# Graph attention layer on one core: where the end of a finished tile stands in the second step, and which engine takes three small operations

## The chip, the cores and the metric

The kernel runs on one core of a Trainium2 chip. A core has five engines with a queue of instructions each: TensorE (PE in the profile; its weight loads are PEld), VectorE (DVE), ScalarE (ACT), GpSimd (POOL) and SyncE (SP), which here only issues DMAs. Every queue is worked in order; the engines wait for one another through semaphores. The metric is the device time of one execution in microseconds (us). Times in nanoseconds are marked ns.

## The reference, cut to what matters

`x` is 3327 x 256, `adj` is 3327 x 3327 and sparse (a few entries in a row). The layer normalises `x`, applies relu, and runs two steps of attention and of diffusion:

```python
def _top_p_attention(X, W1, W2, W3):
    logits = (X @ W1.T @ W2.T) @ (X @ W3.T).T
    probs = softmax(logits)
    # keep the largest entries of a row until they hold TOP_P = 0.9 of its mass
    A = probs * mask
    return A / A.sum(-1, keepdims=True)
R = (S + I) / (S + I).sum(-1, keepdims=True)
for n in range(2):
    A = _top_p_attention(Xa, W1, W2, W3)
    Xf = R @ Xf
    Xa = A @ Xa
    Z = Z + Xf @ U1[n].T + Xa @ U2[n].T
h = X + Z
out = x + (h - h.mean) / sqrt(h.var + 1e-5) * ln_g + ln_b
```

What costs the time is the threshold of the mask: for every row the value above which 90% of the softmax's mass lies, found without sorting.

## The kernel before, in words

The 3327 rows are 26 tiles of 128 (`NT = 26`). Two passes of one loop (`step` 0 and 1) treat every tile; this document calls them the first and the second step. For each tile `t`:

- `weights` (L582 to L610): queries times keys on PE into PSUM, and four `Exp` on ACT (L604, L608, L610) into `e`, 128 x 3328 f32.
- `measured_twice` (L669 to L717, second step): a guess of the threshold, mended twice. Each look at the tile is one pass of ACT over `e` (L633, "ja" in the profile; Relu once and Sign twice, so three passes a tile). Between the passes stand chains of operations on single columns `col(k)` of a small tile `g`: on DVE L685 and L686 after the second pass, L699 and L700 after the third, L716 and L717 at the end; on ACT L687 to L689, L702 to L705, L714; on POOL L690 to L692 and, after the third pass, L697, L698 and L707 to L712. The last six form a ratio of two differences, clamp it and multiply the exponent `col(11)` by it; L714 on ACT uses that.
- `settle` (L725 to L769), DVE: L731 zeroes everything above the guess (a pass over `e` and `e`, with two inputs in SBUF), L736 takes the eight largest of each of 20 segments, L743 and L745 sort out the 40 or 48 largest of these, L750 to L755 find the exact threshold, L765 (L762 in the first and last tile) applies it to `e` and sums; L766 inverts the sum. Then a product of two rows of 40 or 48 elements (L767: on DVE in the first step, on POOL in the second) and its maximum (L769, DVE) go into a record that is only read by a proof at the end.
- `Sums` (L797 to L834): PE transposes `e` in seven parts of four 128 x 128 blocks (L810), ACT copies each part out of PSUM (L812, "eT"), PE multiplies it with the values (L824, "pa").
- `spread` (L1073 to L1090): the sparse diffusion, six matmuls on gathered rows (L911, "pr"; gathers are indirect DMAs issued by POOL, L903) and a closing DVE operation L1086. Its row tile `s1` (four buffers; loaded from memory by L1078) is the tile's result `y` from then on, until it is stored.
- `finish` (L934 to L955, second step): L935 on DVE adds the attention's sum to `y`; L458 and L459 take mean and variance; POOL forms the inverse deviation (L465, L466) and minus mean times it (L943); then POOL adds `bet` to the input's rows `xr` (L945), ACT normalises `y` (L950), POOL multiplies with `gam` (L951) and adds `xr` (L952); SP stores `y` (L955). `xr` has one buffer, which L940 loads.

All these are generators that yield between their pieces. The order of the work is written by hand: `PLAN[1]` (L1104) holds for the second step seven strings, one for each part `k` of a tile's iteration `i`, and each letter advances one generator by one piece: `d` is `settle(i)`, `c` the rest of `settle(i - 1)`, `m` `measured(i + 1)`, `n` the rest of `measured(i)`, `w` `weights(i + 2)`, `q` its start for `i + 3`, `s` `spread(i)`, `g` the gathers for `i + 2`, `f` `finish(i - 2)`, in parts 0 to 3 still `finish(i - 3)`. For the last iterations `LAST` (L1106) replaces the strings. Before the letters of each part the transposes of a part of the sums are put in, after them its matmuls. At the end (L1183) the instructions of PE, ACT, DVE and POOL (POOL from the second step on) are chained in the order of this text, so the plan is the order of execution on each of these engines. SP's queue is not chained: a scheduler orders the DMA issues, and each waits for its own semaphores.

Of the kernel before, what the change touches and what calls it, by code (L numbers as in the profile page):

```python
# [14 lines left out]
ALU = mybir.AluOpType  # L15
# [329 lines left out]
def guess_graph_layer(ctx, tc, x, adj, w1t, w2t, w3t, u1t, u2t, ln_g, ln_b, out, flag):  # L345
# [15 lines left out]
    V, G, S, PE = nc.vector, nc.gpsimd, nc.scalar, nc.tensor  # L361
# [39 lines left out]
    bet = const.tile([P, D], F32, tag="bet", name="bet")  # L401
# [4 lines left out]
    half = const.tile([P, 4], F32, tag="half", name="half")  # L406
# [209 lines left out]
    def guessed(r, g):  # L616

        r["col"] = col = lambda k: g[:, k : k + 1]
        ms = r["ms"]
        S.activation(r["za"], r["za"], AF.Copy, accum_out=r["Z"])  # L620
        S.activation(col(0), r["Z"], AF.Ln)
        S.activation(col(2), col(0), AF.Relu, scale=-0.25, bias=ms(7))
        S.activation(col(2), col(2), AF.Exp, scale=-1.0, bias=con(6))
        S.activation(col(3), col(2), AF.Square, bias=con(3))
        S.activation(col(9), col(3), AF.Exp, scale=ms(3), bias=ms(8))
        return col

    def con(k):
        return one[:, k : k + 1]

    def through(e, f, guess, sign, total):
        ja = scan.tile([P, NP], U8, tag="ja", name="ja")
        S.activation(ja, e, f, bias=guess, scale=sign, accum_out=total)  # L633
# [35 lines left out]
    def measured_twice(r):  # L669
        e, ms = r["e"], r["ms"]  # L670

        col = guessed(r, small.tile([P, 18], F32, tag="g", name="g"))
        S.activation(col(1), col(0), AF.Exp, scale=-1.0, bias=con(5))
        S.activation(col(11), col(2), AF.Square, bias=con(4))
        G.tensor_scalar(col(11), col(11), ms(5), ms(6), ALU.mult, ALU.add)
        G.tensor_scalar(col(5), col(1), OFFSET[1], None, ALU.mult)
        yield
        oa = small.tile([P, 3], F32, tag="oa", name="oa")  # L680
        through(e, AF.Relu, col(9), -1.0, oa[:, 0:1])
        yield
        through(e, AF.Sign, col(9), -1.0, oa[:, 1:2])
        yield
        V.tensor_scalar(col(3), oa[:, 1:2], float(NP), col(9), ALU.add, ALU.mult)  # L685
        V.tensor_scalar(col(4), col(3), 0.5, oa[:, 0:1], ALU.mult, ALU.subtract)  # L686
        S.activation(col(6), col(4), AF.Ln, scale=col(1), bias=con(2))  # L687
        S.activation(col(6), col(6), AF.Exp, scale=col(11))
        S.activation(col(13), col(6), AF.Copy, scale=col(9))  # L689
        G.tensor_scalar(col(14), col(13), col(9), 0.25, ALU.add, ALU.mult)  # L690
        G.tensor_scalar(col(10), col(13), col(5), 1.0, ALU.mult, ALU.add)
        G.tensor_scalar(col(8), col(4), col(1), -1.0, ALU.mult, ALU.add)  # L692
        yield
        through(e, AF.Sign, col(13), -1.0, oa[:, 2:3])
        yield
        d1 = col(17)
        G.tensor_scalar(col(0), oa[:, 2:3], NP - 61.0, BIG, ALU.is_gt, ALU.mult)  # L697
        G.tensor_scalar(col(0), r["Z"], 0.035, col(0), ALU.mult, ALU.add)  # L698
        V.tensor_scalar(col(15), oa[:, 2:3], oa[:, 1:2], col(14), ALU.subtract, ALU.mult)  # L699
        V.tensor_scalar(d1, col(15), col(4), 0.0, ALU.add, ALU.max)  # L700

        S.activation(col(2), d1, AF.Abs, scale=col(1), bias=con(1))  # L702
        S.activation(col(2), col(2), AF.Ln, scale=0.2, bias=col(10))
        S.activation(col(3), d1, AF.Ln, scale=col(1), bias=con(2))
        S.activation(col(2), col(2), AF.Identity, scale=-1.0, bias=col(3))  # L705

        G.tensor_scalar(col(12), col(4), d1, col(1), ALU.subtract, ALU.mult)  # L707
        G.tensor_scalar(col(8), col(8), col(12), None, ALU.mult)
        G.tensor_scalar(col(12), col(12), col(12), 1.0e-12, ALU.mult, ALU.add)
        G.tensor_tensor(col(12), col(12), half[:, 2:3], ALU.pow)  # L710
        G.tensor_scalar(col(12), col(12), col(8), 0.7, ALU.mult, ALU.max)
        G.tensor_scalar(col(11), col(12), 1.5, col(11), ALU.min, ALU.mult)  # L712
        yield
        S.activation(col(3), col(2), AF.Exp, scale=col(11))  # L714
        yield
        V.tensor_scalar(col(6), d1, col(0), BIG, ALU.is_lt, ALU.mult)  # L716
        V.tensor_scalar(col(16), col(3), col(13), col(6), ALU.mult, ALU.add)  # L717
# [7 lines left out]
    def settle(step, t, r):  # L725
        e, col, Z = r["e"], r["col"], r["Z"]
        n = 8 * ROUNDS[step]
        d2 = small.tile([P, 1], F32, tag="d2", name="d2")
        need = small.tile([P, 1], F32, tag="need", name="need")
        w = scan.tile([P, NP], F32, tag="w", name="w")  # L730
        V.scalar_tensor_tensor(w, e, col(16), e, ALU.is_lt, ALU.mult, accum_out=d2)  # L731
        V.tensor_scalar(need, Z, -0.1, d2, ALU.mult, ALU.add)
        yield
        cand = small.tile([P, NSEG * 8], F32, tag="cand", name="cand", bufs=1)
        for s in range(NSEG):
            V.max(cand[:, 8 * s : 8 * s + 8], w[:, s * SEG : min(NP, (s + 1) * SEG)])  # L736
            if s in (NSEG // 2 - 1, NSEG - 1):
                yield
        at = lambda k: rec[:, step, k, t : t + 1]
        V.tensor_reduce(at(0), cand.rearrange("p (s k) -> p s k", k=8)[:, :, 7], AX.X, ALU.max)  # L740
        for k in range(ROUNDS[step]):
            b8 = bb[:, 1 + 8 * k : 9 + 8 * k]
            V.max(b8, cand)  # L743
            if k < ROUNDS[step] - 1:
                V.match_replace(cand, b8, cand, 0.0)  # L745
            if k == 2:
                yield
        b = bb[:, 1 : n + 1]
        cum = small.tile([P, TOPK], F32, tag="cum", name="cum", bufs=1)
        V.tensor_tensor_scan(cum[:, :n], bb[:, :n], bb[:, :n], 0.0, ALU.add, ALU.max)  # L750

        dr = small.tile([P, TOPK], F32, tag="dr", name="dr", bufs=1)
        V.tensor_scalar(dr[:, :n], cum[:, :n], need, None, ALU.is_ge)
        V.scalar_tensor_tensor(cum[:, :n], dr[:, :n], BIG, b, ALU.mult, ALU.add)
        V.tensor_reduce(at(1), cum[:, :n], AX.X, ALU.min)  # L755
        yield
        r["ra"] = ra = small.tile([P, 1], F32, tag="ra", name="ra")
        if t in (0, NT - 1):

            rb = small.tile([P, 1], F32, tag="rb", name="rb", bufs=1)  # L760
            for a, b_, r_ in ((0, FIRST, ra), (FIRST, NP, rb)):
                V.scalar_tensor_tensor(e[:, a:b_], e[:, a:b_], at(1), e[:, a:b_], ALU.is_ge, ALU.mult, accum_out=r_)  # L762
            V.tensor_tensor(ra, ra, rb, ALU.add)
        else:
            V.scalar_tensor_tensor(e, e, at(1), e, ALU.is_ge, ALU.mult, accum_out=ra)  # L765
        V.reciprocal(ra, ra)  # L766
        (G if step else V).tensor_tensor(cum[:, :n], dr[:, :n], b, ALU.mult)  # L767
        yield
        V.tensor_reduce(at(2), cum[:, :n], AX.X, ALU.max)  # L769


# [162 lines left out]
    def finish(t, y, pa, ra):  # L934
        V.scalar_tensor_tensor(y, pa, ra, y, ALU.mult, ALU.add)  # L935
        yield
        mv = spread_of(y)
        yield
        xr = row.tile([P, D], F32, tag="xr", name="xr", bufs=1)
        nc.sync.dma_start(xr, x[t * P : (t + 1) * P])  # L940
        rstd = inverse(mv)
        nm = small.tile([P, 1], F32, tag="nm", name="nm")
        G.tensor_scalar(nm, mv[:, 0:1], rstd, -1.0, ALU.mult, ALU.mult)  # L943
        yield
        G.tensor_tensor(xr, xr, bet, ALU.add)  # L945
        if t == NT - 1:
            V.scalar_tensor_tensor(y, y, mv[:, 0:1], gam, ALU.subtract, ALU.mult)
            V.scalar_tensor_tensor(y, y, rstd, xr, ALU.mult, ALU.add)
        else:
            S.activation(y, y, AF.Identity, bias=nm, scale=rstd)  # L950
            G.tensor_tensor(y, y, gam, ALU.mult)  # L951
            G.tensor_tensor(y, y, xr, ALU.add)  # L952
        yield
        h = min(P, N - t * P)
        nc.sync.dma_start(out[t * P : t * P + h], y[:h])  # L955

# [135 lines left out]
    def refetch(t):  # L1092
# [8 lines left out]


    PLAN = (("mdsssa", "mdsssa", "edawwp", "msda", "mpdea", "gdawwq", "emdgq"),
            ("llcmss", "lnms", "lwwnfd", "lcmdsssg", "fmswqdf", "llmdf", "lmwfd"))  # L1104

    LAST = {NT - 1: ("cfss", "cn", "ndd", "sss", "fddddsf", "f", "f"), NT: ("cf", "", "", "", "ff", "fv", "f"),  # L1106
            NT + 1: ("fv", "f", "", "", "f", "f", "f")}
# [5 lines left out]
    for step in range(2):  # L1113
        sums = Sums(step, live, xw if step else x0, AHEAD[step])

        for i in range(-1, NT + 2):
# [4 lines left out]
            if step == 1 and i == -1:  # L1121
# [5 lines left out]
                n=work["m"],  # L1127
# [9 lines left out]
                b=none, q=none, v=proof() if step and i == NT else work.get("v", none),  # L1137
# [93 lines left out]
```

## Time and profile before

| | us |
|---|---|
| runs: median of three (lowest, highest) | 1406.87 (1405.7, 1407.31) |
| the profiled execution's own time | 1408.79 |
| its span, first to last instruction | 1407.1 |
| DVE busy in the span | 1220.4 (87%) |
| PE busy | 1278.7 (91%) |
| ACT busy | 1105.6 (79%) |
| POOL busy | 989.7 (70%) |
| from 200 to 600, first step, of each 100 us: DVE / PE / ACT / POOL | 96 / 96 / 80 / 70 to 77 |
| from 900 to 1300, second step, of each 100 us: DVE / PE / ACT / POOL | 92 to 94 / 94 to 95 / 94 to 95 / 84 to 87 |
| mean of the granted TensorE clock | 0.974 of full speed |

The profile is that of one execution; 1.7 us of its time lie outside the span. "Busy" is the time in which an engine had an instruction in it, also one that stood still within it. In the listings by time a row gives start, duration, engine, line, operation, tiles (buffer numbers left out) and, where the engine was idle before it, for how long and whose end it then followed. The second step reaches its steady rhythm near 856 us, and keeps it until 1324 us; one tile follows another every 22.2 us.

### The profile page before, as it was taken

The page shows a single profiled execution, that of the slowest core. Times are in us where ns is not written, and L with a number is a line of the kernel's source. Part 1 is how long each engine was busy: PE and PEld are TensorE (multiplying, and loading weights), DVE is VectorE, ACT ScalarE, POOL GpSimd, SP SyncE. Part 2 cuts the span into 40 slices and gives each one's busy share as a digit, 9 for nine tenths or more (in the row PEclk, how much of TensorE's full clock was granted, in tenths as well). Part 3 has the DMA queues.
Part 4 walks back from the last instruction along what each step waited for, and adds up shares of the span by engine and source line. Part 5 has one row for each costly group of instructions (what it writes and reads, how often), then busy time and mean ns, then how long its engine had stood idle before and what let it go on. Part 6 is the DMA issues. An engine that isn't in the chain of part 4 may idle for free.

```text
span 1407.1 us, 22248 instructions
## 1 busy us (share of the span) xinstructions
PE 1278.7 (91%) x6495; PEld 980.9 (70%) x6495; DVE 1220.4 (87%) x3727; ACT 1105.6 (79%) x2423; POOL 989.7 (70%) x1348
## 2 busy tenths in 40 slices
PE   6898999999999999999999479999999999999885
PEld 5545777777777777778786257777777777777664
DVE  6868999999999999998863589999999999999981
ACT  5467887788778788787944689999999999999921
POOL 6214777667667677768862668888888888888832
PEclk9999999999999999999999579999999999999998
DMA  8874454544545445432331202213121221312100
GB/s 284 263 247 126 134 151 133 138 137 135 146 124 148 133 137 152 129 96 73 101 85 57 78 23 79 79 57 90 55 82 58 79 82 54 90 57 79 57 8 22
DMA packets 91203, 149.78 MB, mean 106 GB/s; under 512 B 15265, under 2 KB 58656, under 8 KB 91072
## 3 DMA queue, kind: packets, MB, share of 16 engines
q1 hardware_dynamic: 73616, 105.37, 24.0%
q0 software_dynamic: 16640, 42.69, 12.1%
q8 instruction: 54, 0.88, 0.3%
q14 instruction: 77, 0.63, 0.1%
q10 hardware_dynamic: 816, 0.20, 0.1%
HBM read 120.93 MB, written 27.28 MB: 105 GB/s over the span
## 4 chain that ended last, share of the span: by engine, by line
DVE 51%; PE 24%; ACT 17%; POOL 3%; issue 3%; DMA 1%; DVEq 0%; SPq 0%; POOLq 0%; ACTq 0%
ACT ja L633 11%; DVE e L765 10%; PE pa L824 9%; DVE cand L736 7%; DVE w L731 6%; DVE fm L846 5%; PE pl L600 4%; DVE bb L743 4%; DVE cand L745 4%; PE pt L810 3%; PE pz L988 2%; DVE x L765 2%; ACT eT L812 2%; PE pr L911 1%; ACT e L604 1%
## 5 line engine op out<-in xcount | busy, mean ns | idle before, releaser
L824 PE MATMUL pa<-xw,eT 128*128 128x256 f32 x1352 | 331.9, 387 | 6.6 <-DVE s L935 6.5
L633 ACT ACTIVATE ja<-e,g 128x3328 uint8<-128x3328 f32 x106 | 325.8, 3074 | 0.1
L824 PE MATMUL pa<-x,eT 128*128 128x256 f32 x1352 | 325.2, 382 | 0.0
L824 PEld LDWEIGHTS pa<-xw,eT 128*128 128x128 f32 x1352 | 250.2, 191 | 68.1 <-issue 27.1
L824 PEld LDWEIGHTS pa<-x,eT 128*128 128x128 f32 x1352 | 245.0, 192 | 26.3
L812 ACT COPY eT<-pt 128x512 f32<-128x512 f32 (+1 forms) x364 | 202.1, 556 | 76.6 <-PE pt L810 76.5
L736 DVE MAX8 cand<-w 128x8 f32<-128x168 f32 (+1 forms) x1040 | 251.3, 318 | 0.0
L810 PE MATMUL pt<-ident,e 128*128 128x128 f32 x1144 | 180.7, 278 | 60.6 <-DVE e L765 36.6
L894 POOL DMA_INDIRECT ac<-in_adj,index x130 | 130.7, 1005 | 128.2 <-DVE ms L538 91.2
L810 PEld LDWEIGHTS pt<-ident,e 128*128 128x128 f32 x1144 | 140.7, 144 | 107.3 <-issue 48.1
L903 POOL DMA_INDIRECT xg<-bx,index x130 | 184.8, 1421 | 41.0 <-issue 30.0
L731 DVE SCALAR_TENSOR_TENSOR w<-e,g 128x3328 f32<-128x3328 f32 x44 | 169.1, 3842 | 0.7
L903 POOL DMA_INDIRECT xg<-vx,index x130 | 131.1, 1009 | 45.6 <-issue 33.0
L765 DVE SCALAR_TENSOR_TENSOR e<-e,rec 128x3328 f32<-128x3328 f32 x40 | 156.6, 3915 | 0.7
L911 PE MATMUL pr<-xg,ac 128*128 128x257 f32 (+1 forms) x520 | 139.1, 391 | 11.5 <-DVE s L1086 11.3
L604 ACT ACTIVATE e<-pl 128x832 f32<-128x832 f32 x132 | 113.0, 859 | 36.4 <-PE pl L600 36.3
L911 PEld LDWEIGHTS pr<-xg,ac 128*128 128x128 f32 x520 | 93.9, 195 | 25.1 <-DVE s L1086 11.4
L743 DVE MAX8 bb<-cand 128x8 f32<-128x160 f32 x286 | 92.8, 325 | 6.4
L600 PE MATMUL pl<-after,qT 64*128 64x416 f32 x416 | 96.7, 559 | 0.5 <-ACT qT L528 0.5
L767 POOL TENSOR_TENSOR cum<-dr,bb 128x48 f32<-128x48 f32 x26 | 84.9, 3264 | 15.5 <-DVE rec L755 15.3
L951 POOL TENSOR_TENSOR s<-s,gam 128x256 f32<-128x256 f32 x25 | 92.5, 3701 | 3.2 <-ACT s L950 3.2
L600 PE MATMUL pl<-both,qT 64*128 64x416 f32 x416 | 90.8, 540 | 0.9 <-DVE both L1006 0.9
(259 smaller groups left out, 2210.7 us busy)
## 6 DMA issues: line engine op xcount, KB each, us to landing
at<-in_adj SPq DMA_DIRECT2D x102, 256.0 KB
cx<-ac SPq DMA_DIRECT2D x26, 384.0 KB
ac<-cx SPq DMA_DIRECT2D x26, 384.0 KB
wide<-in_adj SPq DMA_DIRECT2D x10, 832.0 KB
e<-in_adj SPq DMA_DIRECT2D x8, 832.0 KB
bx<-e SPq DMA_DIRECT2D x26, 128.5 KB
own<-bx SPq DMA_DIRECT2D x26, 128.5 KB
x<-in_x SPq DMA_DIRECT2D x13, 256.0 KB
```

The source lines that it names most:

```text
L600: PE.matmul(pl[:, a, :wd], qT[p, :], keys_of(step, a).rearrange("p a b -> p (a b)")[:, c : c + wd], start=True, stop=True)
L633: S.activation(ja, e, f, bias=guess, scale=sign, accum_out=total)
L731: V.scalar_tensor_tensor(w, e, col(16), e, ALU.is_lt, ALU.mult, accum_out=d2)
L736: V.max(cand[:, 8 * s : 8 * s + 8], w[:, s * SEG : min(NP, (s + 1) * SEG)])
L743: V.max(b8, cand)
L765: V.scalar_tensor_tensor(e, e, at(1), e, ALU.is_ge, ALU.mult, accum_out=ra)
L810: PE.transpose(pt[:, j, :], e[:, (j0 + j) * P : (j0 + j + 1) * P], ident)
L812: S.copy(eT[:, :w, :], pt[:, :w, :])
L824: PE.matmul(self.pa, eT[:, c - 4 * k, :], self.xa[:, j, :], start=c == 0, stop=c == NT - 1)
L894: G.indirect_dma_start(out=ac[:, k, :], out_offset=None, in_=rows, in_offset=bass.IndirectOffsetOnAxis(ap=index[:, t, k : k + 1], axis=0), ...
L903: G.indirect_dma_start(out=xg[:, k, :w], out_offset=None, in_=rows, in_offset=bass.IndirectOffsetOnAxis(ap=index[:, t, k : k + 1], axis=0))
L911: PE.matmul(pr[:, :w], ac[:, k, :], own if k == KT - 1 else xg[:, k, :w], start=k == 0, stop=k == KT - 1)
```

## The change

Four edits, all but one in the second step alone:

1. `finish`: the addition of `bet` to `xr` moves from before ACT's normalisation to between the two POOL operations on `y`, and the piece that held the store is joined to the one that normalises.
2. `PLAN[1]`: the last `f` of part 6 goes, so that the next `f`, in part 2 of the next iteration, normalises: ACT's L950 then stands behind the two `w` of that part, and the three POOL operations and the store follow. In part 4 `s` moves ahead of `m`: DVE's L1086 stands before L685 instead of after L686.
3. `measured_twice`: the ratio is formed otherwise. POOL's `col(8)` is now a difference (same count of operations, L692), and the four POOL operations L707 to L710 give way to two on DVE, a difference and a reciprocal, right behind L700. POOL keeps the two clamps.
4. `settle`: the product L767 moves behind the yield, directly ahead of its maximum L769, and is on DVE in both steps. In the first step it was on DVE already; it only moves.

```diff
@@ measured_twice
-        G.tensor_scalar(col(8), col(4), col(1), -1.0, ALU.mult, ALU.add)
+        G.tensor_scalar(col(8), r["Z"], -0.1, col(4), ALU.mult, ALU.add)
         yield
         through(e, AF.Sign, col(13), -1.0, oa[:, 2:3])
         yield
@@
-        G.tensor_scalar(col(12), col(4), d1, col(1), ALU.subtract, ALU.mult)
-        G.tensor_scalar(col(8), col(8), col(12), None, ALU.mult)
-        G.tensor_scalar(col(12), col(12), col(12), 1.0e-12, ALU.mult, ALU.add)
-        G.tensor_tensor(col(12), col(12), half[:, 2:3], ALU.pow)
+        V.tensor_scalar(col(12), col(4), d1, 1.0e-30, ALU.subtract, ALU.add)
+        V.reciprocal(col(12), col(12))
         G.tensor_scalar(col(12), col(12), col(8), 0.7, ALU.mult, ALU.max)
         G.tensor_scalar(col(11), col(12), 1.5, col(11), ALU.min, ALU.mult)
         yield
@@ settle
         V.reciprocal(ra, ra)
-        (G if step else V).tensor_tensor(cum[:, :n], dr[:, :n], b, ALU.mult)
-        yield
+        yield
+        V.tensor_tensor(cum[:, :n], dr[:, :n], b, ALU.mult)
         V.tensor_reduce(at(2), cum[:, :n], AX.X, ALU.max)
@@ finish
-        G.tensor_tensor(xr, xr, bet, ALU.add)
         if t == NT - 1:
+            G.tensor_tensor(xr, xr, bet, ALU.add)
             V.scalar_tensor_tensor(y, y, mv[:, 0:1], gam, ALU.subtract, ALU.mult)
             V.scalar_tensor_tensor(y, y, rstd, xr, ALU.mult, ALU.add)
         else:
             S.activation(y, y, AF.Identity, bias=nm, scale=rstd)
             G.tensor_tensor(y, y, gam, ALU.mult)
+            G.tensor_tensor(xr, xr, bet, ALU.add)
             G.tensor_tensor(y, y, xr, ALU.add)
-        yield
         h = min(P, N - t * P)
         nc.sync.dma_start(out[t * P : t * P + h], y[:h])
@@ PLAN[1]
-            ("llcmss", "lnms", "lwwnfd", "lcmdsssg", "fmswqdf", "llmdf", "lmwfd"))
+            ("llcmss", "lnms", "lwwnfd", "lcmdsssg", "fsmwqdf", "llmdf", "lmwd"))
```

## The prediction

> **What bounds the kernel now.** I read the granted clock first (0.974, so no throttled stage), then busy time by stage, the chain of waits in the second step, and the listing by time of one tile, engine by engine. In the first step DVE is 96% busy and the chain of waits is DVE alone. In the second step DVE, PE and ACT are each 92 to 95% busy and none alone is the bound: the chain goes round all three. One round of it (start, duration, engine, line):
>
> ```profile
> 1076.19 0.21 DVE g L700
> 1076.40 0.24 DVE bb L743
> ...
> 1079.29 4.13 DVE e L765 x2
> ...
> 1083.55 0.63 PE pt L810 x4
> 1084.18 1.60 PE pl L600 x8
> 1085.78 1.92 PE pa L824 x8
> 1087.70 0.45 PE pt L810 x4
> 1088.17 0.59 ACT eT L812
> 1088.76 3.07 ACT ja L633 x2
> ```
>
> From here L685 and L686 on DVE and L687 to L689 on ACT lead to the next "ja", and that to the next L699, 22.2 us after the first. Whatever lengthens a link of this ring costs 22 times over; whatever stands beside it costs nothing until its slack is gone. POOL isn't in the ring, but shows in two of its links. From the listing by time, two steady tiles and, first, one pass that POOL left alone:
>
> ```profile
> 834.13 3.68 DVE L765 SCALAR_TENSOR_TENSOR e<-e,rec 128x3328 f32<-128x3328 f32 x1
> ...
> 1088.17 0.59 ACT L812 COPY eT<-pt 128x512 f32<-128x512 f32 x1 [0.53 <-PE pt L810]
> 1090.91 0.47 DVE L935 SCALAR_TENSOR_TENSOR s<-pa,ra,s 128x256 f32<-128x256 f32 x1
> 1091.85 0.21 DVE L685 TENSOR_SCALAR g<-oa,g 128x1 f32<-128x1 f32 x1 [0.47 <-ACT ja L633]
> ...
> 1101.52 4.10 DVE L765 SCALAR_TENSOR_TENSOR e<-e,rec 128x3328 f32<-128x3328 f32 x1
> 1106.35 4.14 DVE L731 SCALAR_TENSOR_TENSOR w<-e,g 128x3328 f32<-128x3328 f32 x1
> ...
> 1101.41 0.72 POOL L945 TENSOR_TENSOR xr<-xr,bet 128x256 f32<-128x256 f32 x1
> 1102.10 4.11 POOL L951 TENSOR_TENSOR s<-s,gam 128x256 f32<-128x256 f32 x1
> 1106.28 0.73 POOL L952 TENSOR_TENSOR s<-s,xr 128x256 f32<-128x256 f32 x1
> 1106.97 3.65 POOL L767 TENSOR_TENSOR cum<-dr,bb 128x48 f32<-128x48 f32 x1
> ```
>
> L945 starts 0.11 before L765, and L765 takes 4.10 instead of 3.68; L952 does the same to L731. In return L951 and the small L767 stand still until DVE's pass is over.
>
> **What the Trainium skill says.** "SBUF — State Buffer", Who interferes with whom: DVE and GpSimd share a port pair under an exclusive lock; a DVE operation with two SBUF inputs contends with a GpSimd operation that reads SBUF, and the later to issue blocks. The trace agrees (3.68 against 4.10; POOL's 0.72 against 4.11), and shows that DVE gets in between two POOL operations in a row (L945, L765, L951). The same section: a DVE operation with at most one SBUF input doesn't contend. L935 and L1086 read PSUM and one SBUF tile, and keep 0.46 to 0.49 in every tile of the second step. "VectorE: DVE Perf Modes", Rules for kernel authors: keep the count of DVE operations down. Here a dependent single-column operation costs 0.25 start to start (L685 to L686), an independent one 0.13 (L700 to L743).
>
> **The change, part by part** (sums against the span of 1407.1).
>
> *New pair behind L700.* L700 to the difference 0.25, to the reciprocal 0.25, to L743 0.08 (as L766 to L716), together 0.58, where L700 to L743 took 0.13: +0.45 in the ring. The span shows no such pair; between 0.30 (both independent) and 0.65 (0.30 each as L716 to L717). I take 0.45. It is not hidden: only DVE work follows to L765.
>
> *L945 gone from ahead of L765.* L765 to L766 falls from 4.15 to 3.73 (the passes at 834 and 1056, which nothing blocked, show it): -0.42 in the ring. The six POOL operations of the ratio become two, so POOL is idle when L765 starts. Ring so far: +0.03, I carry +0.06, with -0.1 to +0.2 as its ends.
>
> *L950 on ACT*, 0.59. It leaves a place from which everything to the "ja" moves 0.49 earlier, and lands behind two L604, ahead of the eT copy that waits 0.53 for PE. Together it has 0.53 + 0.49 of cover for 0.5: nothing. If the cover were gone, 0.5 a tile.
>
> *L1086 ahead of L685, product on DVE.* Queued behind them are L685, L686 and so ACT's L687 and the third "ja": this is the added wait. From L765's end to L685, DVE has a slack of 0.55 (L935 could hand over 0.39 after its start). L731 without L952: +0.46 slack (L731 to L732 4.19 to 3.73). Product: dependent maximum 0.22 in place of nothing, -0.22. L1086: -0.41. POOL's L951 now waits at L731's end and takes the port first; what that costs the product is seen in the first step, where 11 of 26 products right behind L765 take 0.52 instead of 0.18 while POOL's L928 holds the port: -0.3. Left: about +0.1 of slack. Nothing, then, but close; ends 0 and +0.2. L1086's own inputs are there: the last L911 ends 1.7 before, its `s1` was loaded an iteration ahead.
>
> *POOL and SP.* The three 0.72 additions now follow L731's end and end 2 us later; the five gathers start 0.5 later (they waited for L911 anyway), L690 is then due 2 us before L699 needs it, and L711, L712 have 3 us to L714. The store waits for the last addition; on SP the reload of `xr`, the `ac` of tile i+2 and then `s1` of tile i+1 queue behind it. `ac` slips by 1.3, `s1` waits for the store to land, as before; both are wanted in the next iterations, some 20 us later. Nothing.
>
> *Start of the second step.* Here POOL is in the chain, with L690 behind ten gathers (L903):
>
> ```profile
> 785.65 0.31 POOL L711 TENSOR_SCALAR g<-g 128x1 f32<-128x1 f32 x1
> ...
> 807.24 0.27 DVE L699 TENSOR_SCALAR g<-oa,g 128x1 f32<-128x1 f32 x1 [6.44 <-POOL g L690]
> ...
> 810.78 1.33 POOL L712 TENSOR_SCALAR g<-g 128x1 f32<-128x1 f32 x1
> ```
>
> L711 can start at 784.1 (L700 at 783.36, +0.25, +0.25, +0.16, and 0.1 of semaphore): 1.5 earlier, and with it POOL's laws and ten gathers and L699 at 807.24. In the next chain L712 no longer runs into L762's lock: L714 (812.14) follows ACT's L676 instead, which ends at 811.37, less 1.5: -2.3. ACT's passes, the eT copy that PE waits 6.7 for, and the third "ja" follow, so L699 at 830.71 comes 2.3 earlier, the L765 of 834.13 1.9 (pair +0.45). The next period was 21.83, because nothing blocked L765, and gets the pair too: -1.4 at 855.96.
>
> *Steady tiles:* 22 x 0.06 = +1.3. In 856 to 1346 the trace holds 1.5 us over 22 x 22.22; 0.8 of it is one tile (1056) where L711 ran into L765's lock, and POOL's chain is now too short and early for that. I take 1.5 off; between 0 and 1.5.
>
> *Tail.* At 1351.76 L769, then L716 and L731 wait for POOL's product behind L951 and L952; L731 starts 2.4 after L765's end. After: 1.4, but L765 is still blocked (additions now start there) and carries the pair: -0.6.
>
> *First step.* The product stands 0.7 us or more later, after L928 has gone: 11 x 0.34 = -3.7. Against it the maximum now waits for its product, 0.22 instead of 0.10: 26 x 0.12 = +3.1. -0.6, both ends 1.5 away since lock hits shift (L765 there takes 3.67 to 4.72).
>
> Sum: -1.4 + 1.3 - 1.5 - 0.6 - 0.6 = -2.8; with unrounded terms -2.9. The profiled execution took 1408.79, 1.7 of it outside the span, which the change doesn't touch. Taken off the median of the runs, 1406.87: 1403.9.
>
> **The rivals.** *No change, 1406.* The same ring, but the pair costs 0.55 or L685 is 0.1 late: +0.1 x 22 = +2.2. Nothing in the trace of before speaks against it; the forecast stands on terms of this size.
>
> *Slower, 1417.* The product does not get in after L951 but only after the second addition, which follows with no wait: 0.7 later (L951 to the next POOL operation, as L945 to L951). Less the 0.1 of slack, L685 and the rest of the ring come 0.6 late in each tile: 22 x 0.6 = +13. It makes the kernel slower than before by 0.2% from 0.26 of lateness a tile on (1409.7 less 1403.9, by 22), that is from a hold of the product of about 0.65. For it: nothing but the 0.1 of slack. Against it: L765 got in between L945 and L951 in every tile.
>
> *Faster, near 1393.* POOL (86% busy) is relieved of 1.5 us of the ratio and 3.65 of product a tile; if its blocked time really paced the step, the rhythm could fall to DVE's own work, about 21.7: 22 x -0.5. Against it: POOL itself waits 0.48 for ACT before L697 each tile.
>
> **How the numbers follow.** Small gain as worked out 0.45 (own range 1400 to 1404), large gain 0.05, no change 0.30, slower 0.20, of which half is over 1412. Range 1399 to 1412: it leaves out the large gain and the far half of the slower case. About 0.2%, 2.8 us, is what a measurement of this kernel can tell from no change: faster 0.50, same 0.30, slower 0.20.
>
> **What would show it.** Right: L765 and L731 at 3.68 in steady tiles; L700 to L743 at 0.58; a rhythm of 22.2 to 22.3; L685 still waiting for "ja"; L950 directly before an eT copy; the three POOL operations of the end with about 0.7 each behind L731; L699 near 805.7 at the start; no first-step product of 0.52. Wrong: L685 with no wait, a product of 0.5 or more in steady tiles, a rhythm outside 22.1 to 22.4, or an L731 that waits for POOL.

## The result and the profile after

| | before | after |
|---|---|---|
| median of the runs taken side by side, us (lowest, highest) | 1406.01 (1403.73, 1408.69) | 1406.37 (1403.64, 1409.67) |
| the same again, later | 1406.33 | 1405.78 |
| ratio after to before, 95% interval | | 1.0001 [0.9992, 1.0011]; again 0.9998 [0.9989, 1.0006] |
| the profiled execution, its span | 1408.79, 1407.1 | 1407.77, 1406.0 |
| POOL busy, us | 989.7 | 829.0 |
| steady rhythm of the second step, us a tile | 22.22 | 22.24 |

No difference that can be measured. POOL has lost 161 us of busy time, and the kernel is where it was.

Lines of after are before's less two from L711 on, but for the lines that moved: the mask pass is L763, w L729, the last Exp of the chain L712, the diffusion's sum L1084, the product with `gam` L949. The pair is L707 and L708. First one steady tile of after in the listing by time (start, duration, engine, line, operation, tiles, and in brackets the idle time and what ended it), engine by engine:

```profile
1095.29 0.27 DVE L699 TENSOR_SCALAR g<-oa,g 128x1 f32<-128x1 f32 x1 [0.63 <-POOL rstd L466]
1095.59 0.21 DVE L700 TENSOR_SCALAR g<-g 128x1 f32<-128x1 f32 x1
1095.84 0.21 DVE L707 TENSOR_SCALAR g<-g 128x1 f32<-128x1 f32 x1
1096.09 0.16 DVE L708 RECIPROCAL g<-g 128x1 f32<-128x1 f32 x1
1096.17 0.31 DVE L741 MAX8 bb<-cand 128x8 f32<-128x160 f32 x1
...
1099.14 3.69 DVE L763 SCALAR_TENSOR_TENSOR e<-e,rec 128x3328 f32<-128x3328 f32 x1
...
1103.56 3.69 DVE L729 SCALAR_TENSOR_TENSOR w<-e,g 128x3328 f32<-128x3328 f32 x1
...
1107.42 0.50 DVE L766 TENSOR_TENSOR cum<-dr,bb 128x48 f32<-128x48 f32 x1
...
1110.81 0.48 DVE L1084 SCALAR_TENSOR_TENSOR s<-pr,rrs,s 128x256 f32<-128x256 f32 x1
1111.28 0.21 DVE L685 TENSOR_SCALAR g<-oa,g 128x1 f32<-128x1 f32 x1
...
1094.97 0.21 ACT L633 ACTIVATION_READ_ACCUMULATOR ja<-e,g 128x1 f32 x1
...
1106.45 0.60 ACT L948 ACTIVATE s<-s,nm,rstd 128x256 f32<-128x256 f32 x1
1107.60 0.58 ACT L810 COPY eT<-pt 128x512 f32<-128x512 f32 x1 [0.55 <-PE pt L808]
...
1111.06 0.19 ACT L633 ACTIVATION_READ_ACCUMULATOR ja<-e,g 128x1 f32 x1
...
1107.13 0.72 POOL L949 TENSOR_TENSOR s<-s,gam 128x256 f32<-128x256 f32 x1 [3.78 <-ACT s L948]
1107.81 0.73 POOL L950 TENSOR_TENSOR xr<-xr,bet 128x256 f32<-128x256 f32 x1
```

Both big passes run unblocked (3.69 for 4.10 and 4.14), L700 to the next maximum takes 0.58 for 0.13. L685 follows L1084 and shows no wait, but it still waits for the "ja": it starts 0.03 behind the end of its read-out (1111.06 and 0.19), the same 0.03 as before, where the listing shows a wait of 0.47. Now L1084's row covers that wait. L685 starts 0.47 after L1084 started; in "two products" below, where the "ja" has long ended, it starts 0.39 after it. So about 0.08 of slack is left. The normalisation stands under the cover of the wait for PE, and POOL's work comes behind w.

The bracket behind L699 names POOL's L466, and the chain of waits of after believes it; there the path no longer goes through DVE and PE but through POOL's gathers:

```profile
1094.38 0.26 POOL rstd L465
...
1094.71 0.58 POOL rstd L466
1095.29 0.28 DVE g L699
```

That link isn't real. L466 makes the inverse deviation of another tile, which L699 doesn't read; it reads the third "ja", whose read-out ended at 1095.18 (1094.97 and 0.21). The median start of L699 is 0.11 behind that read-out in all fourteen profiles, before's too. The two ends lie 0.1 apart, and the later one was named. The run with four POOL operations below has the same L699 with L466 finished 0.3 ahead of it.

Where the time went, from the start of one mask pass to another. The first step ends at the second piece of its last tile's mask pass, the start of the second at tile 2's; "steady" are the 21 periods from there to tile 23's, and the last row runs to the end of the last DVE operation, 9.2 ahead of the span's end:

| stretch | before | after | after again | predicted difference | measured |
|---|---|---|---|---|---|
| up to the first mask pass | 112.73 | 114.19 | 113.55 | 0 | +1.5, +0.8 |
| first step | 609.77 | 607.77 | 607.70 | -0.6 | -2.0, -2.1 |
| start of the second | 133.46 | 131.61 | 131.69 | -1.4 | -1.9, -1.8 |
| steady | 467.66 | 467.83 | 467.80 | -0.2 (+1.3 - 1.5) | +0.2, +0.1 |
| last tiles to the end | 74.23 | 75.41 | 75.47 | -0.6 | +1.2, +1.2 |

The change cannot reach the first row: over the fourteen profiles of this study it lies between 111.5 and 114.2. The 326th of POOL's 390 gathers tells why the steady part gave almost nothing back for its odd tile. Before, then after:

```profile
1043.51 0.23 POOL L678 TENSOR_SCALAR g<-g 128x1 f32<-128x1 f32 x1
1045.47 1.12 POOL L903 DMA_INDIRECT xg<-vx,index  x1 [1.72 <-PE pt L810]
...
1056.51 3.60 POOL L711 TENSOR_SCALAR g<-g 128x1 f32<-128x1 f32 x1
```

```profile
1040.97 0.73 POOL L951 TENSOR_TENSOR s<-s,xr 128x256 f32<-128x256 f32 x1
1044.34 1.10 POOL L901 DMA_INDIRECT xg<-vx,index  x1 [2.64 <-PE pq L523]
...
1050.78 0.27 DVE L699 TENSOR_SCALAR g<-oa,g 128x1 f32<-128x1 f32 x1 [1.52 <-POOL g L690]
```

In the other steady tiles of these two kernels POOL stands idle for 0.16 to 0.29 before the first gather of a tile.

### The profile page after: what moved, and what is told of

It reads as the page before. It is cut to its first block, busy times and chain, and to the rows that moved or that the text cites. A ratio compares the mean times of both kernels' runs of the same rounds, so it can differ in the third digit from the quotient of the medians.

```text
span 1406.0 us, 22193 instructions
## 1 busy us (share of the span) xinstructions
PE 1279.7 (91%) x6495; PEld 982.5 (70%) x6495; DVE 1222.8 (87%) x3805; ACT 1105.2 (79%) x2423; POOL 829.0 (59%) x1218
## 4 chain that ended last, share of the span: by engine, by line
DVE 40%; PE 23%; ACT 18%; POOL 11%; issue 5%; DMA 1%; POOLq 0%; SPq 0%; ACTq 0%; DVEq 0%
PE pa L822 9%; DVE cand L734 7%; POOL xg L901 7%; ACT ja L633 6%; DVE w L729 6%; DVE e L763 5%; DVE fm L844 5%; PE pl L600 3%; PE pt L808 3%; DVE cand L743 3%; DVE bb L741 2%; PE pz L986 2%; PE pr L909 2%; ACT eT L810 2%; DVE x L763 2%
## 5 line engine op out<-in xcount | busy, mean ns | idle before, releaser
L901 POOL DMA_INDIRECT xg<-bx,index x130 | 193.1, 1485 | 40.8 <-issue 28.8
L729 DVE SCALAR_TENSOR_TENSOR w<-e,g 128x3328 f32<-128x3328 f32 x44 | 162.5, 3693 | 0.7
L763 DVE SCALAR_TENSOR_TENSOR e<-e,rec 128x3328 f32<-128x3328 f32 x40 | 149.8, 3745 | 0.7
L677 POOL TENSOR_SCALAR g<-g,law 128x1 f32<-128x1 f32 x23 | 47.1, 2049 | 86.9 <-ACT g L676 86.9
L741 DVE MAX8 bb<-cand 128x8 f32<-128x160 f32 x286 | 92.6, 324 | 6.4
L844 DVE TENSOR_REDUCE fm<-at 128x4 f32<-128x512 f32 (+1 forms) x119 | 75.4, 634 | 0.0
```

What stands on the lines that cost most here:

```text
L844: V.tensor_reduce(fm[:, j0 : j0 + n], at[:, :n], AX.X, ALU.max, apply_absolute_value=True)
L901: G.indirect_dma_start(out=xg[:, k, :w], out_offset=None, in_=rows, in_offset=bass.IndirectOffsetOnAxis(ap=index[:, t, k : k + 1], axis=0))
```

## The experiments

The theory after the result: +0.45 for the pair and -0.42 for the freed port lie in the same ring and cancel; all else is beside it. The first four kernels were made to take the two terms apart.

**The ratio back on POOL.** After, with edit 3 undone (the six operations of before, and `col(8)` as before):

```diff
-        V.tensor_scalar(col(12), col(4), d1, 1.0e-30, ALU.subtract, ALU.add)
-        V.reciprocal(col(12), col(12))
+        G.tensor_scalar(col(12), col(4), d1, col(1), ALU.subtract, ALU.mult)
+        G.tensor_scalar(col(8), col(8), col(12), None, ALU.mult)
+        G.tensor_scalar(col(12), col(12), col(12), 1.0e-12, ALU.mult, ALU.add)
+        G.tensor_tensor(col(12), col(12), half[:, 2:3], ALU.pow)
```

> The kernel after, with the ratio back on POOL in its six operations of before and nothing else undone. Theory (the pair costs 0.45 in the ring, and it alone eats what the freed port gives): L700 to the next maximum 0.13 instead of 0.58, rhythm 22.24 - 0.45 = 21.8, time 1406 - 23 x 0.45 = about 1396. Rival A (the pair is hidden, or the two terms weren't what cancelled; something else holds the rhythm at 22.2): 1404 to 1407. Rival B (the longer ratio ends only 0.1 before the mask pass, as in the kernel before; being in the way of the lock it is blocked through the pass in every tile, and ACT's Exp with the third ja behind it): L712 3 us or more, the Exp about 1.2 late, rhythm about 23, time about 1420.

Measured: 1432.04, ratio 1.0182 [1.0165, 1.0199], rhythm 23.55. Rival B, 12 us over its figure. The listing by time (before's line numbers here):

```profile
1088.09 0.27 DVE L699 TENSOR_SCALAR g<-oa,g 128x1 f32<-128x1 f32 x1 [0.63 <-ACT ja L633]
...
1091.51 3.69 DVE L765 SCALAR_TENSOR_TENSOR e<-e,rec 128x3328 f32<-128x3328 f32 x1
...
1089.09 0.25 POOL L697 TENSOR_SCALAR g<-oa 128x1 f32<-128x1 f32 x1
...
1091.77 3.60 POOL L711 TENSOR_SCALAR g<-g 128x1 f32<-128x1 f32 x1
...
1095.81 0.29 ACT L714 ACTIVATE g<-g 128x1 f32<-128x1 f32 x1 [1.85 <-POOL g L712]
```

A POOL operation on one column that starts 0.26 after the mask pass stands still through the whole mask pass, and ACT's queue behind L714 with it. Before, L697 began 0.02 ahead of L699 and L712 was done 0.08 ahead of the mask pass. With the end behind w, POOL's three operations of the end stand before the gathers, the gathers before L697, and L697 comes 1.0 behind L699. So the two main edits aren't independent: the long ratio doesn't fit in once the end has moved.

**The ratio alone.** Before with edit 3 only (the same lines the other way round).

> The kernel before with the ratio's pair on DVE alone; the end of a tile and the small product stay as before. Theory: +0.45 in the ring, while the shorter ratio lets POOL's addition (bet) go before the mask pass, but its product with gam still waits for ACT's normalisation (end 101.4 where the mask pass starts at 101.97 on the clock of the tile shown), so the mask pass stays blocked for 0.1 to 0.4: rhythm 22.4 to 22.65, start about 1.5 to 2 us earlier; time 1408 to 1414. Rival (the pair is hidden): 1404 to 1406, rhythm 22.2 or less.

Measured: 1409.17, ratio 1.0025 [1.0013, 1.0038], rhythm 22.40: as the theory had it. The pair costs 0.44, and the mask pass, at 3.84, gets 0.27 back, since POOL's addition of `bet` starts 2.1 ahead of it instead of 0.1, and only the product with `gam`, which starts 0.36 ahead, still delays it:

```profile
1101.79 3.84 DVE L763 SCALAR_TENSOR_TENSOR e<-e,rec 128x3328 f32<-128x3328 f32 x1
...
1101.43 0.72 POOL L949 TENSOR_TENSOR s<-s,gam 128x256 f32<-128x256 f32 x1 [1.03 <-ACT s L948]
```

**The end alone.** Before with edit 1 and the `f` of part 6 taken out, nothing else.

```diff
-            ("llcmss", "lnms", "lwwnfd", "lcmdsssg", "fmswqdf", "llmdf", "lmwfd"))
+            ("llcmss", "lnms", "lwwnfd", "lcmdsssg", "fmswqdf", "llmdf", "lmwd"))
```

> The kernel before with the end of a tile moved behind the next w alone; ratio, small product and the place of the diffusion's sum stay as before. Theory: mask pass 3.68 and w pass 3.69 as after, no pair: rhythm 22.22 - 0.42 = 21.8, time about 1397; it differs from the kernel after with the ratio on POOL by no more than 2 us, since the small product and the sum's place lie beside the ring. Rival (moving the end costs what it frees, by ACT's normalisation or POOL's late additions): 1404 to 1407. Rival (ratio blocked by the mask pass in every tile): about 1420.

Measured: 1431.34, ratio 1.0181 [1.0164, 1.0198], rhythm 23.54: the second rival, 11 us over its figure. The mask pass starts at 1090.59, and L711 meets it:

```profile
1090.74 3.70 POOL L711 TENSOR_SCALAR g<-g 128x1 f32<-128x1 f32 x1
```

It equals the first experiment within 1 us, so the small product and the place of the sum are beside the ring here.

**Four columns.** After with two more reciprocals behind the pair (`V.reciprocal(col(12), col(12))` twice).

> The kernel after with two more reciprocals in a row behind the pair (the value is the same but for rounding). Theory: each dependent single-column operation there costs 0.25 in the ring, so L700 to the maximum 1.08, rhythm 22.74, time 1406 + 23 x 0.5 = about 1418. Rival (operations there are partly hidden, by the wait of the next step for ACT or PE): 1406 to 1410, rhythm 22.2 to 22.4.

Measured: 1416.62, ratio 1.0068 [1.0051, 1.0085], rhythm 22.64. Each of the two costs 0.20 a tile, not the 0.25 expected, and all of it arrives. Nothing hides an operation there.

**Two products.** After with the small product made twice.

```diff
         V.tensor_tensor(cum[:, :n], dr[:, :n], b, ALU.mult)
+        V.tensor_tensor(cum[:, :n], dr[:, :n], b, ALU.mult)
```

> The kernel after with the small product made twice in a row on DVE behind L730 (same result). Theory (L685 has no slack left after the change, it follows the diffusion's sum with no wait): everything by which the second product delays L685 goes into the rhythm once a tile: 0.2 if it gets the port at once, 0.8 if POOL's second addition, which starts 0.14 before it, shuts it out; rhythm 22.45 to 23.05, time 1411 to 1425. Rival (there is slack that the profile doesn't show, L685 isn't a link of the ring): 1404 to 1408, rhythm 22.24.

Measured: 1423.86, ratio 1.0122 [1.0101, 1.0144], rhythm 22.85. The listing by time (the added line is L767, and what follows is higher by one):

```profile
1095.06 0.51 DVE L766 TENSOR_TENSOR cum<-dr,bb 128x48 f32<-128x48 f32 x1
1095.60 0.66 DVE L767 TENSOR_TENSOR cum<-dr,bb 128x48 f32<-128x48 f32 x1
...
1095.47 0.72 POOL L951 TENSOR_TENSOR xr<-xr,bet 128x256 f32<-128x256 f32 x1
```

The second product is shut out by POOL's second operation of the end, the addition of `bet`, and 0.61 of its 0.69 arrives in every tile. The missing 0.08 is the slack that L685 had: L1085 to L685 now takes 0.39, where after has 0.47. The expectation took the slack for zero; it is 0.08.

**The sum back.** After with `s` behind `m` again in part 4.

```diff
-            ("llcmss", "lnms", "lwwnfd", "lcmdsssg", "fsmwqdf", "llmdf", "lmwd"))
+            ("llcmss", "lnms", "lwwnfd", "lcmdsssg", "fmswqdf", "llmdf", "lmwd"))
```

> The kernel after with the diffusion's sum back behind L686, where it was before. Theory (in the kernel after L685 comes just as the ja ends, so its slack is used up but the ring isn't lengthened): L685 again waits 0.3 to 0.4 for the ja, rhythm 22.20 to 22.24, time within 1.5 of after's. Rival (the sum's place costs in the ring): rhythm 21.8 to 22.1, time 1396 to 1403.

Measured: 1405.75, ratio 0.9996 [0.9986, 1.0007], rhythm 22.24; L685 waits 0.38 for the "ja". As expected: the sum ahead of L685 costs nothing; it uses up all of the slack but the 0.08.

**The variance behind the ratio.** The first experiment with `f` moved from part 5 to part 1, so that L465, L466 and L943 stand behind the six operations. (The plan of the last tiles wasn't adapted, so the end of one tile is left out, and the total is short of it; the rhythm isn't.)

```diff
-            ("llcmss", "lnms", "lwwnfd", "lcmdsssg", "fsmwqdf", "llmdf", "lmwd"))
+            ("llcmss", "lnfms", "lwwnfd", "lcmdsssg", "fsmwqdf", "llmd", "lmwd"))
```

> The kernel after with the ratio in its six POOL operations, as in the run with the ratio on POOL, but the three POOL operations of the variance (rstd and nm) and the load of xr moved from ahead of the ratio to behind it. Theory (there the ratio came too late because the moved end stands ahead of the gathers: L697 0.46 behind L699 in the kernel after where it was 0.02 ahead in the kernel before, the last ratio operation then starts 3.58 behind L699, and the mask pass 3.42): L697 follows the ja again, the last ratio operation ends 3.34 behind L699, 0.08 ahead of the mask pass; rhythm 21.8 to 22.0 (the upper end if rstd's first operation delays the mask pass), time 1396 to 1401. Rival (the ratio is blocked by the lock all the same, by another 0.1 of lateness): rhythm 23.5, time 1430. Rival (the pair on DVE wasn't what cost): 1404 to 1407.

Measured: 1416.92, ratio 1.0069 [1.0050, 1.0089], rhythm 22.71; none of the three. L697 is 0.02 ahead of L699 again and L712 gets through, as expected. But:

```profile
1088.63 3.96 POOL L466 TENSOR_TENSOR rstd<-rstd,half 128x1 f32<-128x1 f32 x1
...
1093.00 0.60 ACT L950 ACTIVATE s<-s,nm,rstd 128x256 f32<-128x256 f32 x1 [1.08 <-POOL nm L943]
```

L466 starts 0.15 after w (1088.48) and falls under its lock, the normalisation waits for `nm`, and the second "ja" behind it on ACT is late. The wait had moved to the next small operation.

**The ratio in four.** After, with the pair as a difference and a power on POOL:

```diff
-        V.tensor_scalar(col(12), col(4), d1, 1.0e-30, ALU.subtract, ALU.add)
-        V.reciprocal(col(12), col(12))
+        G.tensor_scalar(col(12), col(4), d1, 1.0e-30, ALU.subtract, ALU.add)
+        G.tensor_tensor(col(12), col(12), half[:, 2:3], ALU.pow)
```

> The kernel after with the pair on POOL as a difference and a power of -1 (four POOL operations for the ratio in place of six before and two after), nothing else changed; the ratio's sign is kept only if the power takes a negative base. Theory: no pair in the ring and the ratio still clear of the lock (0.37, 0.57, 0.34, 0.30 with 0.1 between: last one starts 2.6 to 2.8 behind L699, the mask pass 3.42): rhythm 21.8, start of the second step within 0.5 of after's, time about 1396. Rival (the pair is not what holds the rhythm): 1404 to 1407. Rival (blocked as the six were): about 1430. If the power fails on negative bases, the guess fails and the second, exact program runs behind the first: over 2000, and nothing follows for the others.

Measured: 1395.88, ratio 0.9913 [0.9891, 0.9934], rhythm 21.80: the theory.

```profile
1093.01 0.27 DVE L699 TENSOR_SCALAR g<-oa,g 128x1 f32<-128x1 f32 x1 [0.62 <-ACT ja L633]
1093.32 0.21 DVE L700 TENSOR_SCALAR g<-g 128x1 f32<-128x1 f32 x1
1093.45 0.32 DVE L741 MAX8 bb<-cand 128x8 f32<-128x160 f32 x1
...
1096.45 3.69 DVE L763 SCALAR_TENSOR_TENSOR e<-e,rec 128x3328 f32<-128x3328 f32 x1
...
1092.10 0.57 POOL L466 TENSOR_TENSOR rstd<-rstd,half 128x1 f32<-128x1 f32 x1
...
1095.28 0.31 POOL L710 TENSOR_SCALAR g<-g 128x1 f32<-128x1 f32 x1
```

L707 to L710 on POOL end 0.86 ahead of the mask pass, and the pair is out of the ring: L700 to L741 is 0.13 again. (L466 is the operation that the chain of waits of after named; here L699 starts 0.34 after its end.)

**Four alone.** Before with this ratio, and nothing else.

> The kernel before with the ratio in four POOL operations and nothing else of the change. Theory (the gain needs the end moved: POOL's product with gam still waits for ACT's normalisation, which ends as the mask pass starts): the addition (bet) goes 0.8 earlier, but the product with gam then stands against the mask pass; mask pass 3.8 to 4.1, rhythm 21.9 to 22.2, time 1399 to 1406. Rival (the shorter ratio alone frees the port): mask pass 3.68, rhythm 21.8, time 1396 to 1398.

Measured: 1409.24, ratio 1.0018 [1.0011, 1.0025], rhythm 22.40: the mask pass stays blocked, as the theory had it, but the kernel is slower than either side expected.

```profile
1099.75 0.55 DVE L751 TENSOR_SCALAR dr<-cum,need 128x48 f32<-128x48 f32 x1
...
1100.81 3.98 DVE L763 SCALAR_TENSOR_TENSOR e<-e,rec 128x3328 f32<-128x3328 f32 x1
...
1099.53 0.73 POOL L943 TENSOR_TENSOR xr<-xr,bet 128x256 f32<-128x256 f32 x1
1100.59 0.73 POOL L949 TENSOR_TENSOR s<-s,gam 128x256 f32<-128x256 f32 x1 [0.33 <-ACT s L948]
```

The addition of `bet`, now 1.3 ahead of the mask pass where it was 0.1, runs into DVE's L751 (0.55 for 0.25), the product with `gam` into the mask pass. The shorter ratio alone loses 0.2%; with the end behind w it gains 10 us.

**The last end.** After, with one end of a tile, that of tile 22, behind the last w:

```diff
-    LAST = {NT - 1: ("cfss", "cn", "ndd", "sss", "fddddsf", "f", "f"), ...
+    LAST = {NT - 1: ("css", "cn", "nddf", "sss", "fddddsf", "f", "f"), ...
```

> The kernel after with the end of the last tile but two (normalisation, three POOL operations, store) behind the last w instead of ahead of the last but one mask pass. Theory (POOL's three operations there lengthen two small DVE operations by 0.42 and 0.46 and the mask pass by 0.26): these three at 0.25, 0.21 and 3.68, last period 1.1 shorter than after's 24.43, the end of the program 0.5 to 1.1 earlier; time 1404.5 to 1406. Rival (the reload of xr behind the store comes late for the last tiles): end no earlier or up to 2 later. The rest of the second step as after.

Measured: 1403.53, ratio 0.9984 [0.9977, 0.9991]. After, at the last mask pass but one:

```profile
1344.18 0.67 DVE L751 TENSOR_SCALAR dr<-cum,need 128x48 f32<-128x48 f32 x1
1344.89 0.67 DVE L752 SCALAR_TENSOR_TENSOR cum<-dr,bb 128x48 f32<-128x48 f32 x1
...
1345.83 3.94 DVE L763 SCALAR_TENSOR_TENSOR e<-e,rec 128x3328 f32<-128x3328 f32 x1
...
1344.08 0.73 POOL L949 TENSOR_TENSOR s<-s,gam 128x256 f32<-128x256 f32 x1 [1.23 <-ACT s L948]
1344.77 0.72 POOL L950 TENSOR_TENSOR xr<-xr,bet 128x256 f32<-128x256 f32 x1
1345.57 0.72 POOL L951 TENSOR_TENSOR s<-s,xr 128x256 f32<-128x256 f32 x1
```

With the end moved:

```profile
1341.81 0.25 DVE L751 TENSOR_SCALAR dr<-cum,need 128x48 f32<-128x48 f32 x1
1342.09 0.21 DVE L752 SCALAR_TENSOR_TENSOR cum<-dr,bb 128x48 f32<-128x48 f32 x1
...
1342.57 3.69 DVE L763 SCALAR_TENSOR_TENSOR e<-e,rec 128x3328 f32<-128x3328 f32 x1
```

The three rows are as expected, and the time is 1.0 below the range expected: the last tiles take 73.21 instead of 75.41, twice the 1.1 that these three rows hold. The other half comes after the last mask pass. There the granted clock stood at half for 3.4 us from 1350.7 and for 6.8 us from 1371.1 in after, and only for 3.4 us from 1368.9 here; that this makes up the other half isn't shown.

**Both.** The ratio in four and the last end together.

> The kernel after with the two corrections together: the ratio in four POOL operations (rhythm 21.8, 1395.9 by itself) and the end of the last tile but two behind the last w (2.8 less than after by itself). They touch different stretches, so the gains should add: 1393 to 1394. Rival (the end of the program is held by something else once the rhythm is faster, such as loads or the PE work of the last tile): 1395 to 1397.

Measured: 1395.96, ratio 0.9924 [0.9911, 0.9938]. Faster than both kernels, but the expected 1393 to 1394 did not come; the time lies in the rival's range, and the medians show nothing on top of the ratio in four. The rival's reason isn't shown either: in the profile the last tiles take 73.00 for 74.53. The two intervals overlap, and 1.5 us is within them.

**After again**, unchanged:

> The kernel after once more, unchanged, to weigh the small terms: in the first profiles it stood 1.5 later than before at the first mask pass already, where the change has not acted, and gained 2.0 in the first step, 1.85 in the start of the second, and gave back 1.2 at the end. If the late begin was chance, the median comes out 1 to 2.5 below before's; if the kernels are really equal, within 1 of it. In the profile: first step (first mask pass to the last) 607.7 to 608.4 as in the five runs with the product on DVE behind the next work, against 609.2 to 609.8 with the old order; last period 24.4; POOL's 326th gather 2.6 late.

Measured: 1405.78, ratio 0.9998 [0.9989, 1.0006]: equal. The stretches behind the first repeat to 0.1 (the table above).

What the eleven kernels say of the ring, in medians over thirteen steady tiles (the numbers of a row sum to its rhythm within 0.03):

| kernel | L699 to mask pass | mask pass | its end to L685 | L685 to L699 | rhythm |
|---|---|---|---|---|---|
| before | 3.42 | 4.11 | 8.46 | 6.25 | 22.22 |
| after | 3.85 | 3.68 | 8.46 | 6.25 | 22.24 |
| ratio alone | 3.86 | 3.84 | 8.46 | 6.24 | 22.40 |
| four columns | 4.25 | 3.68 | 8.45 | 6.25 | 22.64 |
| two products | 3.85 | 3.68 | 9.07 | 6.24 | 22.85 |
| the sum back | 3.85 | 3.68 | 8.45 | 6.25 | 22.24 |
| ratio on POOL | 3.44 | 3.69 | 10.18 | 6.25 | 23.55 |
| end alone | 3.42 | 3.68 | 10.18 | 6.25 | 23.54 |
| variance behind | 3.41 | 3.69 | 9.41 | 6.20 | 22.71 |
| four alone | 3.71 | 3.99 | 8.46 | 6.25 | 22.40 |
| ratio in four | 3.42 | 3.68 | 8.45 | 6.24 | 21.80 |

## Why the prediction was right and wrong

The range held; the likeliest case, a small gain, did not come. The time is that of the rival "no change", but not by its reasons: neither did the pair cost 0.55 nor did L685 lengthen the ring. That the total fits is in part luck: against the profiles the tail missed upwards by 1.8 and the steady tiles by 0.4, the first step downwards by 1.4 and the start by 0.5.

- *The ring.* Right to within 0.02. The pair +0.43 (predicted +0.45), the port -0.43 (-0.42), the ring +0.02 (+0.03 worked out, +0.06 carried). "Ratio in four" takes the pair away alone and gives 21.80.
- *L685.* Right. The prediction left it "about +0.1 of slack"; 0.08 is left. Two of the marks set for "wrong" seemed to appear: the product of 0.5 did, with the hold of 0.3 that the sum had allowed for; L685 with no wait is so in the listing alone. From the mask pass's end to L685 it is 8.46 before and after, set by the "ja" both times. The slower rival's mechanism is real: a DVE product that meets the addition of `bet` is shut out, and its delay beyond the 0.08 goes into each tile ("two products"), only here the one product gets in ahead of it.
- *Steady tiles, "I take 1.5 off".* This step failed. The trace of before showed L711 under the lock in the tile at 1056, and I took the lock for the cause. Behind it stands the late 326th gather, which no edit removes: POOL stands idle before it in all fourteen profiles, and L697 and the ratio come a microsecond late. After, the lock is gone, but L699 waits 1.52 for L690 in the same tile, and its period is 23.17 where it was 23.04. Over the steady tiles 0.2 of the 1.5 came. In several of the experiments one or two tiles behind it stumble too; in four of them the granted clock is at half for 3.4 us there.
- *Tail, "-0.6".* Failed, by 1.8. I counted the wait for POOL's product as gone, which it is, and left out where the last plan puts the moved end: ahead of the last mask pass but one, where POOL's three operations run into L751, L752 and L763 (+1.1). "The last end" shows it. This was to be had from the order of the instructions. In that period L699 also stands 0.8 later than the freed port would have it, at a "ja" whose eT copy waits for PE. Before, then after:

```profile
1335.76 2.49 PE L824 MATMUL pa<-xw,eT 128*128 128x256 f32 x8 [2.48 <-DVE s L935]
```

```profile
1333.19 3.43 PE L822 MATMUL pa<-xw,eT 128*128 128x256 f32 x8 [2.55 <-DVE s L933]
```

The granted clock is at half for 3.4 us in both, from 1337.12 before and from 1333.58 after; within it one of these matmuls takes 0.63 instead of 0.38. Before, 2.0 of the 3.4 lie ahead of the end of the transposes that the copy waits for, after all of it: at half speed an estimated 1.0 and 1.7 lost, which is most of the 0.8. What lowers the clock there isn't shown.
- *Start of the second step, "-1.4".* The first part is right: L699 at 805.18 follows L690, and counted from the end of the first step it comes 1.5 earlier, as worked out. The rest of the measured -1.9 can't be told apart from the clock, which from 808 on is at half for 17.1 us before and for 13.7 after. "The sum back" has 17.1 too, and though its L699 stands within 0.2 of after's, tile 1's mask pass comes 1.7 later than after's; which of the two follows from the other is open.
- *First step, "-0.6".* Mis-sized. Kernels with the product behind the next work take 607.7 to 608.4 from the first mask pass to the last, three with the old order 609.2 to 609.6, before 609.8: about -1.6. The products at 0.52 are gone as expected, so the +3.1 for a maximum that waits was probably too much: by difference it is about 2, which no run shows by itself. "Two products" (612.4: 26 further products, 4.5) shows that every 0.17 counts there.
- *POOL, SP, normalisation: nothing.* Right.
- *The clock, "no throttled stage".* Misread: 0.974 is the mean of the span. By stage it is 0.77 from 750 to 800, 0.89 from 800 to 900 and 0.90 from 1350 on, and the terms for the start and the tail lie there.
- *What the prediction didn't see.* That the edits lean on each other: it summed them as parts, and no part said that the end behind w pushes L697 behind L699, so that the six operations would be caught by the mask pass. The move needs a shorter ratio; the pair on DVE is the dearer of the two that were tried. The faster rival's time of 1393 came within 3 us in "both", but by the pair, not by POOL's load.

What stays open: the stretches of the profiles give after 2.5 us less than before if the first row is left out, the runs 0 with an interval of about 1.3 to either side. One profile of before stands against two of after, and the difference is of the size of the scatter at the beginning. What the clock does in the start and in the tail adds to it.

## To carry to other kernels

An engine's idle time isn't a place for work as long as that work stands in a queue ahead of something short that has a deadline: here three operations put six others on one column each behind a lock, and 0.3 us of lateness cost 1.7 us a tile (10.18 for 8.46 in the table). Before an operation is moved to another engine, ask whether the first one can do it in fewer operations; the ratio in four POOL operations kept the 10 us that the pair on DVE, a link of the ring, gave away again. When an odd tile is to be explained away, look for its first late instruction, not for its longest one. A row that shows no wait can still have waited, under the end of the row before it: compare its start with the end of what it reads. And read the clock by stage, not as a mean.

## What I hadn't expected of the hardware

- POOL's 326th gather is late in all fourteen profiles: it starts 1.72 after the operation ahead of it in before, 2.46 to 2.64 in the others, at any time from 1038 to 1057. Against the other tiles of the same kernel (0.29 in before, 1.0 in "ratio alone" and "four alone", 0.17 in the rest) that is 1.4 to 1.5 more where the end stands in its old place and about 2.5 more where it has moved. Two more first gathers of steady tiles are late, 6.73 in "ratio alone" and 5.12 in "four alone"; the others start after 0.15 to 1.0. The cause is in none of the views.
- One POOL operation on one column (L711, 0.34 unblocked) took 3.60 to 3.70 when it started 0.15 to 0.26 after the mask pass. "SBUF — State Buffer", Who interferes with whom, has it that the later to issue blocks for the whole of the other; the runs agree, and show it for 1, 48 and 256 columns alike (3.60 here, 3.65 for the small product and 4.11 for the product with `gam` in before).
- A DVE operation of 128 x 48 with one input tile (L751) takes 0.55 to 0.67 instead of 0.25 beside a POOL operation on two SBUF tiles. The same section says that `tensor_scalar` can take the shared pair too, in a mode of two ports; that this one did is inferred from its time. The prediction quoted the rule for one SBUF input without this exception.
- A dependent reciprocal of one column costs 0.20 from start to start, a `tensor_scalar` 0.25.
- A power with exponent -1 on POOL takes 0.56 for 128 x 1.
